# Queries read the state at their block's end; biases move into a last weight row; one gelu activation per expert block

## The chip, the cores and the metric

The kernel runs on one core of one Trainium2 chip, in one launch. A core has five engines that each work through an instruction queue of their own, in order: TensorE (PE in the profile) multiplies matrices into PSUM, VectorE (DVE) and ScalarE (ACT) work on SBUF and PSUM, GpSimd (POOL) works on SBUF and issues indirect DMAs, SyncE (SP) issues the other DMAs. They wait for each other through semaphores. The metric is the device time of an execution in microseconds (us), all data in float32.

## The reference

Input x has 8 sequences of 512 steps with 128 features. Two layers follow each other, each as attention and feed-forward part with a residual connection, each part fed with a layer norm of x (mean removed, divided by the standard deviation, no gain).

```python
x = x + ssm(_layernorm(x))          # gated linear recurrence along the steps
x = x + (_layernorm(x) @ W[idx] + b[idx])   # one of 8 matrices, picked from logits
x = x + delta(_layernorm(x))
x = x + moe(_layernorm(x))
```

The third is the delta rule. With 16 heads of 8 features, each step and head updates a state S of 8x8 and reads it after the update:

```python
normed = (x - mu) * rsqrt(var + LN_EPS) * ln_g + ln_b
q, k, v, beta_pre = split(normed @ w_qkvb + b_qkvb)   # k is then normalised
def step(S, inp):
    q_t, k_t, v_t, beta_t = inp
    retrieval = einsum('bhij,bhj->bhi', S, k_t)
    S = S + einsum('bhi,bhj->bhij', beta_t * (v_t - retrieval), k_t)
    o_t = einsum('bhij,bhj->bhi', S, q_t)
    return (S, o_t)
out = x + scan_out @ w_out + b_out
```

The fourth is a mixture of experts. A router (128x8) and softmax pick two of eight experts for each of the 4096 rows; an expert is `gelu(x @ w1 + b1) @ w2 + b2` with 512 hidden features, and the two results are added with the softmax weights.

## The kernel before

**Tiles and stages.** The 512 steps are cut into 32 tiles of 16 steps; a tile holds the 8 sequences of these steps, 128 rows. Eight chunks of 4 tiles go through the stages: `first_layers` (the first part in `scanned` and `ssm_out`, the second in `linear`), `delta_in` (norm, q, k, v, beta and per-block matrices of the delta rule), `delta_rule`, `route` (router). Chunks are gathered into groups of 1, 2, 2, 2 and 1 (`GROUPS`), and `experts` runs once for each group.

**The order** is written out: every operation is first recorded with a number, and `ORDER`, a table of numbers, says in which order they are emitted (`ordered`, line 189), so on each engine's queue too. Which PSUM bank an operation gets follows in `ordered` from which one was free longest. Because operations go through a recorder, most instructions carry its line, L335, in the profile; groups are told apart by their tiles.

**The delta rule.** A tile is worked in four blocks of 4 steps, 128 blocks in all, one after the other, since each needs the state that the one before leaves. Rows of SBUF are (head, feature) pairs. The state and the terms added to it lie in PSUM (`st`, two banks in turn). A block is six instructions on DVE (lines 1308 to 1337): the product `so` = (queries, keys of this block) x state, 128x512; its reduction over the key features, with the values already written beside it, gives `w`, value less retrieval; a product with a 4x4 matrix for each sequence and head (`tmat`, made in `delta_in` from keys and beta) and its reduction give the four steps' updates `u`; keys times `u` into `st`, and its reduction is the next state. Keys carry the minus sign that is needed.

The queries' half of `so` is q times the state at the block's *start*. What the updates inside the block add to a step's output is made up by correction planes `qkp`: dot products of a step's query with the keys of the steps of its block, four planes (own step, others), made in `delta_in` on POOL (products), PE (sums over a head's features with `head_ones`) and ACT (copies into `qk_planes`). POOL multiplies them with the updates shifted against each other (`upd`), and PE adds the eight planes of `so` and the four of `qkp` times `wo` into the tile's output; from tile 8 on POOL first adds the planes of `so` in pairs, and from tile 28 on the `qkp` planes onto them (`PRESUM`). DVE then adds the result to `base` and has x3.

Keys and queries reach the block's layout by way of DRAM: `scratch<-knq` stores a chunk, `kq<-scratch` loads a tile, keys and queries apart, each copied to the eight rows of a head; `kq` has two buffers.

**Biases.** In `linear` the chosen bias `bsel` is added to x1 on POOL, and DVE adds the product in PSUM to it. In `experts` w1 and b1 are copied in DRAM into `w1b_dram`, rows of 516 numbers: 512 weights and 4 columns of bias.

**Experts.** DVE computes each row's place in a table sorted by expert. POOL scatters the normed rows (`places<-xne`, 128 rows per indirect DMA). A group of n tiles takes 15 (n = 4) or 23 (n = 8) blocks of 128 rows, 99 in all. For a block SP loads the expert's `w1b` (four buffers), PE makes four 128x128 products `ph`, ACT four gelus of 128x128, each with its bias column, and PE four products with w2 (`po<-w_sb,hid`, or `in<-`). Four blocks' results are stored, POOL gathers them back by row (`back<-results`), multiplies with the weights and adds (`fin`) for the chunks of the first three groups; for the last two groups DVE does this in one instruction per tile. `out_rows` then goes to the output.

Of the kernel before, what the change touches and what calls it, by code (L numbers as in the profile page):

```python
# [16 lines left out]
P = 128  # L17
# [52 lines left out]
class Plan:  # L70
# [118 lines left out]
    def ordered(self):  # L189

        order, loaded, freed = [], None, list(range(-len(self.banks), 0))
        for at, number in enumerate(ORDER):
            op = self.ops[number]
            for b in op.begins:
                b.index = min(b.choice, key=freed.__getitem__)
                freed[b.index] = len(ORDER)
            for b in op.ends:
                b.users -= 1
                if b.users == 0:
                    freed[b.index] = at  # L200
            switch = op.table if op.table and op.table != loaded else None
            loaded = switch or loaded
            order.append((op, switch))
        return order
# [154 lines left out]
def _cost(engine, name, n, kw):  # L359
# [28 lines left out]
    0, 9, 63, 116, 57, 1, 11, 69, 67, 40, 3, 18, 46, 4, 13, 61, 2, 5, 32, 44, 8, 23, 62, 48, 6, 7, 59, 49, 22, 29,  # L388
    20, 330, 411, 50, 75, 109, 12, 15, 70, 45, 16, 17, 51, 43, 110, 54, 47, 71, 10, 26, 41, 68, 72, 111, 27, 33, 112,
    14, 19, 60, 325, 113, 25, 337, 73, 42, 21, 35, 114, 65, 115, 24, 34, 117, 64, 125, 331, 118, 119, 74, 344, 126,  # L390
    127, 120, 323, 36, 124, 128, 132, 79, 133, 121, 52, 122, 53, 135, 123, 338, 129, 134, 351, 130, 76, 37, 131, 137,
    136, 39, 326, 358, 139, 138, 365, 327, 78, 328, 140, 141, 142, 89, 84, 90, 148, 149, 147, 143, 86, 329, 150, 154,
    155, 144, 145, 157, 151, 146, 156, 152, 153, 159, 158, 382, 161, 160, 379, 163, 164, 162, 380, 165, 171, 169,
    170, 28, 381, 383, 172, 166, 177, 176, 384, 167, 168, 179, 178, 385, 173, 386, 174, 181, 175, 180, 387, 182, 183,
    87, 333, 80, 185, 186, 332, 388, 446, 184, 334, 191, 335, 77, 187, 193, 192, 81, 389, 336, 199, 188, 352, 194,
    189, 390, 190, 200, 198, 195, 203, 196, 197, 201, 391, 58, 392, 204, 202, 208, 106, 91, 340, 205, 108, 207, 85,
    209, 206, 345, 88, 213, 31, 396, 214, 210, 215, 211, 107, 221, 393, 212, 83, 38, 216, 220, 416, 394, 395, 858,
    217, 222, 398, 218, 223, 92, 225, 219, 399, 224, 226, 93, 397, 227, 339, 400, 229, 94, 228, 366, 230, 235, 30,
    236, 237, 55, 56, 231, 359, 401, 243, 242, 372, 238, 232, 402, 233, 245, 234, 244, 403, 239, 240, 247, 241, 95,
    246, 96, 404, 341, 248, 249, 97, 98, 251, 252, 99, 342, 250, 253, 100, 101, 258, 259, 257, 254, 415, 260, 255,  # L400
    66, 405, 264, 265, 102, 256, 267, 266, 261, 406, 262, 269, 263, 268, 104, 270, 447, 271, 103, 354, 273, 274, 407,
    448, 272, 451, 275, 279, 449, 280, 82, 452, 276, 281, 287, 277, 105, 278, 453, 286, 408, 282, 288, 289, 409, 283,
    284, 291, 285, 290, 410, 292, 293, 450, 353, 413, 295, 347, 355, 454, 294, 356, 296, 455, 297, 412, 299, 346,
    460, 298, 348, 417, 414, 349, 418, 456, 461, 466, 300, 462, 420, 303, 301, 304, 467, 308, 305, 302, 457, 309,
    468, 312, 421, 313, 310, 422, 306, 423, 311, 314, 307, 419, 357, 469, 315, 316, 458, 317, 350, 373, 343, 318,
    367, 424, 360, 319, 320, 368, 459, 321, 322, 470, 361, 483, 324, 463, 425, 427, 464, 471, 579, 426, 375, 428,
    374, 429, 440, 465, 430, 431, 432, 435, 433, 436, 434, 472, 437, 438, 439, 362, 363, 441, 369, 442, 473, 443,
    444, 445, 474, 514, 581, 513, 475, 376, 515, 516, 517, 377, 482, 518, 476, 519, 523, 520, 477, 529, 521, 530,
    522, 478, 531, 526, 532, 378, 527, 480, 525, 533, 524, 364, 583, 534, 479, 580, 484, 370, 481, 536, 485, 535,
    537, 582, 487, 542, 538, 539, 528, 544, 540, 543, 541, 545, 548, 550, 546, 553, 551, 584, 585, 549, 586, 587,  # L410
    646, 554, 588, 488, 489, 490, 547, 555, 491, 648, 556, 561, 492, 647, 494, 557, 507, 558, 1193, 493, 689, 371,
    690, 495, 562, 593, 496, 486, 559, 563, 552, 560, 565, 564, 497, 566, 574, 498, 567, 594, 568, 569, 595, 570,
    649, 500, 502, 575, 650, 571, 599, 591, 572, 499, 573, 651, 501, 652, 503, 653, 600, 504, 505, 654, 592, 601,
    655, 656, 657, 658, 602, 659, 660, 506, 661, 603, 508, 662, 589, 663, 664, 509, 665, 510, 590, 666, 511, 667,
    668, 675, 732, 669, 676, 688, 512, 677, 730, 596, 678, 604, 576, 1128, 1127, 597, 679, 670, 680, 671, 577, 681,
    672, 616, 673, 731, 691, 578, 598, 682, 674, 692, 693, 1130, 694, 695, 605, 683, 696, 684, 685, 697, 1129, 686,
    1131, 698, 699, 606, 687, 700, 1132, 701, 1133, 1137, 702, 1134, 703, 1143, 607, 1144, 704, 705, 1140, 706, 608,
    1141, 707, 1136, 708, 1135, 709, 615, 609, 710, 1145, 717, 774, 1196, 711, 718, 712, 1146, 772, 719, 713, 1197,
    720, 714, 721, 1147, 722, 773, 733, 715, 610, 1148, 734, 716, 735, 736, 723, 737, 724, 1149, 738, 725, 1150, 726,
    739, 611, 740, 1151, 741, 613, 742, 743, 727, 1152, 744, 614, 745, 1153, 1156, 746, 1154, 747, 728, 748, 1155,  # L420
    1157, 617, 1138, 729, 1158, 1164, 749, 1167, 1195, 1165, 750, 1194, 1162, 751, 1159, 752, 612, 759, 1160, 753,
    760, 754, 761, 1163, 762, 755, 1168, 763, 1262, 756, 1161, 764, 765, 775, 1169, 1139, 766, 1261, 1198, 757, 1199,
    776, 1170, 1175, 618, 758, 1260, 1200, 1201, 1171, 1166, 777, 1202, 767, 778, 768, 779, 769, 1207, 780, 1176,
    781, 770, 1177, 782, 1172, 1208, 783, 620, 1209, 784, 785, 1173, 786, 1179, 1203, 1213, 787, 1174, 788, 1178,
    1214, 1205, 789, 1204, 1180, 790, 791, 792, 1181, 793, 1182, 794, 801, 1304, 1183, 771, 802, 1302, 795, 803,
    1184, 621, 796, 804, 797, 805, 1185, 798, 622, 799, 1303, 806, 1186, 1263, 623, 624, 619, 807, 1264, 1187, 808,
    1206, 625, 1215, 626, 1188, 1536, 627, 800, 1265, 1216, 1266, 1267, 628, 640, 814, 809, 1268, 1190, 1269, 1142,
    629, 1217, 810, 1270, 1189, 1271, 1211, 630, 1272, 634, 1273, 1274, 631, 1210, 1218, 1275, 635, 632, 1276, 633,
    1277, 636, 1278, 1212, 637, 1279, 638, 811, 1280, 639, 1281, 1219, 1191, 1282, 641, 642, 1346, 1283, 812, 1284,
    1289, 643, 1285, 1290, 1286, 1291, 1537, 1345, 644, 1305, 1292, 1287, 1293, 1220, 1294, 1306, 1295, 1307, 645,  # L430
    1221, 1308, 1230, 1470, 1538, 1222, 1309, 1539, 813, 1296, 1192, 1310, 1540, 1541, 1288, 1471, 1542, 1223, 1543,
    1311, 1544, 1473, 1472, 1312, 1224, 1297, 1313, 1298, 1474, 1314, 1545, 1315, 1225, 1316, 1550, 815, 1344, 1226,
    1317, 816, 1299, 1318, 1227, 1475, 1319, 1479, 1320, 1321, 1478, 1228, 1322, 817, 1551, 1323, 1556, 1229, 1324,
    1331, 1388, 1552, 1325, 1332, 1326, 1333, 1557, 1300, 1327, 1334, 818, 1335, 1476, 1328, 1387, 1336, 1558, 1386,
    1337, 1231, 1329, 1338, 1477, 1546, 1232, 1330, 1559, 1486, 1487, 1488, 819, 1489, 1347, 1234, 1339, 1560, 1340,
    1348, 1341, 1490, 1342, 1349, 1350, 1233, 1572, 1351, 1547, 1480, 1235, 1352, 1236, 1237, 1353, 1238, 1354, 822,
    1355, 1548, 1561, 1239, 1481, 1241, 1499, 2282, 1240, 1549, 1356, 1242, 1357, 1491, 1554, 1358, 1359, 1553, 1243,
    1360, 1493, 1361, 1492, 1362, 1254, 1363, 1555, 1364, 1494, 1365, 1500, 1562, 1366, 1495, 1367, 1373, 1507, 1368,
    1374, 1496, 1369, 1573, 1370, 1371, 1244, 1483, 1375, 1343, 1372, 1376, 1389, 1497, 1377, 1378, 1245, 1390, 1379,
    1380, 1498, 1563, 1605, 1391, 1381, 1392, 1382, 1393, 1383, 1384, 1564, 1394, 1512, 823, 1508, 1395, 1484, 1396,  # L440
    1565, 2286, 1397, 820, 1301, 1398, 1246, 1510, 1385, 1566, 1399, 1501, 1400, 1247, 1401, 821, 1604, 1509, 824,
    1567, 1402, 825, 826, 1568, 1403, 1404, 1511, 827, 1405, 1406, 1570, 1482, 828, 1407, 1502, 829, 830, 831, 1408,
# [1444 lines left out]
```

## Time and profile before

| | us |
|---|---|
| time, median of 3 (lowest to highest) | 690.27 (689.65 to 692.26) |
| the profiled execution, own time | 689.16 |
| its span, first to last instruction | 687.4 |
| mean granted TensorE clock | 0.868 |
| first and last `so` product begin | 99.5 and 561.6 |
| last reduction of the delta rule ends | 565.0 |
| last output of a tile added to x3 | 576.1 |
| last scatter of rows begins | 621.8 |

The profile lists busy time by engine and by groups of like instructions: engine, operation, what is written from what, shapes and count, then total busy us and mean ns of one, then idle time ahead of them with what ended it. PEld is TensorE's loading of weights, beside PE. A float32 product counts as two PE records. The longest groups of each engine are, in us busy: PE `ph<-xbT,w1b` 124.5, ACT `hid<-ph,w1b` 116.4, DVE `so<-kq,st` 87.8 and the two reductions of the delta rule 63.7 and 63.0, POOL the scatter 63.0 and the gather 61.3. A wait named in the profile is the one that ended last.

### The profile page before, as it was taken

How to read it: one execution, taken by the hardware profiler on the slowest of the kernel's cores; microseconds unless marked ns; L12 is line 12 of the kernel's file. 1: busy time of each engine (PE TensorE's matmuls, PEld its weight loads, DVE VectorE, ACT ScalarE, POOL GpSimd, SP SyncE). 2: the span in 40 equal slices, each digit the busy share in tenths (PEclk: the TensorE clock that was granted, in tenths of full speed). 3: DMA queues.
4: the chain of work that ended last, by engine and by line, in shares of the span. 5: the costliest groups of instructions: out<-in, count | busy, mean ns of one | idle time of the engine just before them, and what ended most of it. 6: DMA issues, size and time to landing. Idle time of an engine off the chain costs nothing. (4 is left out here: it accounts for less than half of the span.)

```text
span 687.4 us, 10830 instructions
## 1 busy us (share of the span) xinstructions
PE 513.5 (75%) x2948; PEld 402.5 (59%) x2948; DVE 504.4 (73%) x1351; ACT 480.3 (70%) x1129; POOL 484.3 (70%) x522
## 2 busy tenths in 40 slices
PE   4976575776667786894779787886988788969960
PEld 3763233444435454583748565765778787969850
DVE  5786759989999989988699999997899970300121
ACT  2565687757786779897698799966878457836640
POOL 4164563695589879698869886976788687774443
PEclk9966577888987589988799979997999899999995
DMA  3894062343242654656268666564697767877761
GB/s 88 248 263 136 0 169 62 103 110 78 61 108 61 186 137 122 157 146 161 80 155 234 164 153 178 151 191 145 179 242 206 207 189 214 272 210 219 223 197 46
DMA packets 94977, 107.48 MB, mean 156 GB/s; under 512 B 8667, under 2 KB 68006, under 8 KB 94918
## 3 DMA queue, kind: packets, MB, share of 16 engines
q1 hardware_dynamic: 89616, 97.97, 52.4%
q0 software_dynamic: 4160, 8.53, 4.3%
q8 instruction: 25, 0.41, 0.3%
q10 hardware_dynamic: 1142, 0.29, 0.2%
q14 instruction: 34, 0.28, 0.2%
HBM read 84.93 MB, written 27.61 MB: 164 GB/s over the span
## 5 line engine op out<-in xcount | busy, mean ns | idle before, releaser
L335 ACT ACTIVATE hid<-ph,w1b 128x128 f32<-128x128 f32 x396 | 116.4, 380 | 45.3 <-PE ph L335 29.2
L335 PE MATMUL ph<-xbT,w1b 128*128 128x128 f32 x792 | 124.5, 287 | 18.5 <-DMA w1b<-w1b_dram 12.7
L335 PEld LDWEIGHTS ph<-xbT,w1b 128*128 128x128 f32 x792 | 108.0, 199 | 31.9 <-issue 17.9
L1601 PE MATMUL po<-w_sb,hid 128*128 x608 | 98.4, 284 | 5.2 <-ACT hid L335 4.2
L1601 PEld LDWEIGHTS po<-w_sb,hid 128*128 128x128 f32 x608 | 85.0, 198 | 14.5 <-ACT hid L335 8.0
L335 DVE TENSOR_TENSOR so<-kq,st 128x512 f32<-128x512 f32 x128 | 87.8, 686 | 6.7 <-PE po L335 2.0
L335 POOL DMA_INDIRECT back<-results,small_dest x64 | 61.3, 958 | 38.8 <-issue 15.9
L1539 POOL DMA_INDIRECT places<-xne,small_dest x64 | 63.0, 984 | 18.9 <-issue 14.3
L304 ACT ACT_TABLE_LOAD x56 | 71.8, 1283 | 1.0
L335 DVE TENSOR_REDUCE st<-st 128x64 f32<-128x320 f32 x128 | 63.7, 498 | 3.8
L335 DVE TENSOR_REDUCE st<-so 128x32 f32<-128x320 f32 x128 | 63.0, 492 | 4.0
L335 PE MATMUL po<-wo,so 128*128 128x128 f32 x248 | 49.7, 331 | 20.9 <-DVE so L335 10.1
L335 PEld LDWEIGHTS po<-wo,so 128*128 128x128 f32 x248 | 43.3, 239 | 31.1 <-DVE so L335 12.5
L335 DVE TENSOR_TENSOR st<-kq,st 128x256 f32<-128x256 f32 x128 | 54.6, 426 | 3.6
L335 POOL TENSOR_TENSOR qkp<-qkp,upd 128x512 f32<-128x512 f32 x32 | 38.9, 1215 | 15.3 <-ACT upd L335 12.9
L335 PE MATMUL in<-b,wqkvb 128*128 128x512 f32 x64 | 41.0, 741 | 9.6 <-ACT b L335 4.3
L335 PE MATMUL in<-f,wT 128*128 128x512 f32 x64 | 42.3, 756 | 7.1 <-ACT f L335 3.8
L335 DVE SCALAR_TENSOR_TENSOR fin<-back,small_weight,fin 128x128 f32<-128x128 f32 x16 | 5.0, 351 | 56.7 <-DMA w1b<-w1b_dram 44.1
L335 POOL TENSOR_TENSOR f<-f,f 128x512 f32<-128x512 f32 x24 | 30.4, 1273 | 19.9 <-ACT f L335 19.9
L335 DVE TENSOR_REDUCE st<-prod 128x32 f32<-128x128 f32 x128 | 37.5, 293 | 7.8 <-ACT upd L335 2.4
L335 POOL TENSOR_TENSOR so<-so 128x512 f32<-128x512 f32 x24 | 30.5, 1271 | 13.2 <-PE in L335 6.4
L335 DVE TENSOR_TENSOR prod<-tmat,st 128x128 f32<-128x128 f32 x128 | 36.6, 286 | 4.0
(300 smaller groups left out, 1301.0 us busy)
## 6 DMA issues: line engine op xcount, KB each, us to landing
kq<-scratch SPq DMA_DIRECT2D x64, 512.0 KB
w1b<-w1b_dram SPq DMA_DIRECT2D x99, 258.0 KB
xb<-places SPq DMA_DIRECT2D x21, 256.0 KB
results<-yb SPq DMA_DIRECT2D x21, 256.0 KB
scratch<-knq SPq DMA_DIRECT2D x16, 256.0 KB
places<-yb SPq DMA_DIRECT2D x2, 1472.0 KB
w1b_dram<-in_L_ffn_w_dram SPq DMA_DIRECT2D x1, 2048.0 KB
u_rows<-in_L_attn_u_dram SPq DMA_DIRECT2D x7, 256.0 KB
```

The costliest lines, as they stand in the source:

```text
L304: self.hw.scalar.preload_act_table_set(switch)
L335: return method(*(on(x) for x in args), **{k: on(x) for k, x in kw.items()})
L1539: rows_out = hw.gpsimd.indirect_dma_start(out=table[0 : nblk * P, :], out_offset=bass.IndirectOffsetOnAxis(ap=at, axis=0), in_=src, in_off ...
L1601: return hw.tensor.matmul(out_.on(nc.banks), lhsT=src, rhs=w2_f[:, bass.ds(at + c * P, P)], start=(c == 0), stop=(c == NHB - 1),)
```

## The change

1. **The delta rule's order within a block.** `so` is computed at the block's end, from the state after its updates. The queries in it are this block's, the keys those of the *next* block, whose retrieval it prepares. So the stored keys and values are shifted by one block (`STEP` = 32 columns): a chunk's keys go to `scratch` in three stores, 96 columns of them into the last tile's place, and the next chunk's first 32 columns complete that tile. `first_keys` and `first_block` provide for the first block, and the very last `so` has queries alone. `delta_in` of a chunk is recorded one chunk earlier than before.
2. **Three correction planes.** With the state read at the end, the own step needs none, and later steps of the block are subtracted: planes 0 to 2, with a minus sign, and updates shifted the other way. The product of queries and keys on POOL, its 128x512 product on PE and its copy on ACT are gone, and a tile's output adds three `qkp` planes (one, from tile 28 on).
3. **Biases.** A normed row sums to zero, so its last feature is minus the sum of the others. The last weight row is subtracted from the other 127 (`differences`, a product with `less_last`), the last feature is set to 1, and the bias becomes the last row: for w1 and `wr` (no bias there) and `wsel`. For w1 this is done once at the start: 1 MB each into the two `kq` buffers, eight products of 128x512, copies by DVE and ACT, a store to `w1b_dram`, and b1 over every last row. `w1b` has rows of 512 numbers.
4. **x2** is made, from the second chunk on, by adding x1 in PSUM with an identity product and one copy on ACT, in place of DVE's addition.
5. **Gelu** of a block is one activation of 128x512.
6. **Weighting** of gathered rows for the first three groups is done by ACT, 128x128 each, instead of POOL.
7. `ORDER` is another one, and the banks are listed in `BANKS`.

```diff
@@ ordered
-        order, loaded, freed = [], None, list(range(-len(self.banks), 0))
+        order, loaded, banks = [], None, iter(BANKS)
...
-                b.index = min(b.choice, key=freed.__getitem__)
...
+                b.index = int(next(banks))
@@ setup
+    def differences(src):
+        pt = mm_tile()[:, 0 : src.shape[1]]
+        nc.tensor.matmul(pt, lhsT=less_last, rhs=src, start=True, stop=True)
+        return pt
...
-    nc.sync.dma_start(w1b_dram[:, 0 : NHB * P], w1.rearrange("e d f -> (e d) f"))
...
+    for h in range(2):
+        w1_sb = ptile([P, half_e, FW], "kq", 2)
+        nc.sync.dma_start(w1_sb, w1[h * half_e : (h + 1) * half_e].rearrange("e p f -> p e f"))
+        for e in range(half_e):
+            copied = nc.scalar.copy if e % 2 else nc.vector.tensor_copy
+            copied(w1_sb[:, e], differences(w1_sb[:, e]))
+        nc.sync.dma_start(
+            w1b_dram[h * half_e * P : (h + 1) * half_e * P].rearrange("(e p) f -> p e f", p=P), w1_sb
+        )
+    nc.sync.dma_start(w1b_dram.rearrange("(e p) f -> e p f", p=P)[:, P - 1, :], b1)
...
+    nc.tensor.matmul(pt, lhsT=less_last, rhs=wsel, start=True, stop=False)
+    nc.tensor.matmul(pt, lhsT=only_last, rhs=bsel, start=False, stop=True)
+    nc.vector.tensor_copy(wsel, pt)
@@ linear
-        x1b = ptile([P, n, D], "f", FIRST)
-        nc.gpsimd.tensor_add(x1b, x1, over_tiles(bsel, n))
+        xn = ptile([P, n, D], "f", FIRST)
+        nc.gpsimd.memset(xn[:, :, D - 1 :], 1.0)
+        normalised(x1, rstd, shift, tiles_of(xn[:, :, 0 : D - 1]), leads=leads)
...
-        nc.vector.tensor_add(x2, tokens_out(xT, wsel), x1b)
+        if leads:
+            nc.vector.tensor_add(x2, tokens_out(xT, wsel), x1)
+        else:
+            nc.scalar.copy(x2, tokens_out(xT, wsel, onto=x1))
@@ delta_in
+        before_first = scratches[(g - 1) % 2][1, SIZES[g - 1] - 1, :, QN - STEP :] if g else first_keys
+        nc.sync.dma_start(before_first, kn[:, 0:STEP])
+        nc.sync.dma_start(tiled(scratch[0, 0:NT]), qn.rearrange("p (q c) -> p q c", c=QN))
+        nc.sync.dma_start(
+            tiled(scratch[1, 0 : NT - 1]), kn[:, STEP : STEP + (NT - 1) * QN].rearrange("p (q c) -> p q c", c=QN)
+        )
+        nc.sync.dma_start(scratch[1, NT - 1, :, 0 : QN - STEP], kn[:, STEP + (NT - 1) * QN :])
...
-        nc.gpsimd.tensor_mul(pa, qn, kn)
...
-        nc.scalar.copy(planes[:, 3, :], project_md(head_ones, pa))
@@ delta_rule, in a block
-                nc.vector.tensor_mul(so_v[:, :, :, ts], kq_v[:, :, ts], state)
-                nc.vector.tensor_reduce(w.rearrange("p b t -> p (b t)"), so_r[:, ts], AX.XY, ALU.add)
+                so_r = so_before[:, DH * QN :].rearrange("p (x c e) -> p c x e", c=QN, e=2)
+                nc.vector.tensor_reduce(w.rearrange("p b t -> p (b t)"), so_r[:, before_], AX.XY, ALU.add)
...
                 nc.vector.tensor_reduce(terms(n + 1)[:, :, BL], sum_n, AX.X, ALU.add)
+                so_before, k_before = now, keys_of(kq)
+                sides_ = 1 if last and k == QB - 1 else 2
+                state = terms(n + 1)[:, :, BL].unsqueeze(1).unsqueeze(3).to_broadcast([P, sides_, DH * B, BL])
+                xs = slice(0, sides_ * DH // 2)
+                nc.vector.tensor_mul(so_v[:, xs, :, ts], kq_v[:, 0 : sides_ * DH, ts], state)
@@ delta_rule, after a tile
-                outs += [mine[:, d, :] for d in range(BL)]
+                outs += [mine[:, d, :] for d in range(BL - 1)]
@@ experts
-            for c in range(NHB):
-                cs = slice(c * P, (c + 1) * P)
-                nc.scalar.activation(
-                    hid[:, cs], ph[:, cs], AF.Gelu_apprx_tanh, bias=w1b[:, NHB * P + c : NHB * P + c + 1]
-                )
+            nc.scalar.activation(hid, ph, AF.Gelu_apprx_tanh)
...
-                    weight = weights[:, c].unsqueeze(2).to_broadcast([P, n, D])
-                    nc.gpsimd.tensor_mul(back[c], back[c], weight)
+                    for i in range(n):
+                        nc.scalar.mul(back[c][:, i], back[c][:, i], weights[:, c, i : i + 1])
@@ the chunks' loop
+    x2s = {g: first_layers(g) for g in range(2)}
+    delta_ready(0)
+    first_block(ready[0][1])
+    for g in range(NG):
+        if g + 1 < NG:
+            delta_ready(g + 1)
```

## The prediction

> **What bounds the kernel now.** The engine totals come first: no engine fills the span, so shares decide nothing and the stages have to be found.
>
> ```profile
> span 687.4 us, 10830 instructions
> PE 513.5 (75%) x2948; PEld 402.5 (59%) x2948; DVE 504.4 (73%) x1351; ACT 480.3 (70%) x1129; POOL 484.3 (70%) x522
> DVE  5786759989999989988699999997899970300121
> ```
>
> The DVE row of the forty slices (17.2 us each) has three parts: six slices of setup, a plateau of eights and nines to slice 33, then almost nothing. The plateau is the delta rule. Its first `so` product starts at 99.5, its last reduction ends at 565.0 (timeline of DVE). Busy time in four stretches, cut where the delta rule begins and ends, where PE hands out the last tile (575.9) and where PE's last expert block ends (666):
>
> ```profile
> core 0: us, PE busy (x) PEld busy (x) DVE busy (x) ACT busy (x) POOL busy (x), PEclk, DMA share, GB/s
> 99.00:563.00 464.00, 356.74 (x1985) 273.30 (x1985) 418.40 (x1058) 358.96 (x799) 360.88 (x387) 0.87 0.55 147
> 563.00:575.90 12.90, 10.09 (x84) 9.61 (x85) 2.16 (x6) 6.26 (x22) 11.05 (x14) 1.00 0.71 201
> 575.90:666.00 90.10, 79.15 (x653) 75.30 (x651) 13.01 (x57) 58.00 (x180) 54.44 (x55) 0.98 0.78 227
> 666.00:687.40 21.40, 1.12 (x2) 0.29 (x2) 3.32 (x9) 0.56 (x2) 7.56 (x8) 0.58 0.25 71
> ```
>
> In the plateau DVE is busy 418.4 of 464.0 us, PE, ACT and POOL 77 to 78%. From 575.9 to 666 PE leads, 79.2 of 90.1 us. The last 21.4 us are results, gathers and stores. The list of DVE's waits in the plateau says what DVE lacks:
>
> ```profile
> DVE x L335 <- PE in L335: 9.5, 5, 2.7
> DVE x L335 <- PE po L335: 2.9, 1, 2.9
> DVE st L335 <- ACT upd L335: 2.4, 1, 2.4
> DVE so L335 <- PE po L335: 2.0, 2, 1.2
> ```
>
> Columns are total us, times, longest. With the entries under 1 us these are 19.1 us. The other 26.5 of the 45.6 idle us are some 25 ns after each of 1058 instructions. So the plateau is a DVE stage with little to squeeze except work removed from DVE and these waits, and the tail is a PE stage whose length is the number of expert blocks still to do.
>
> **The recurrence, part by part.** One of the 128 steps is six DVE instructions: `so` 0.686, reduction of `so` 0.492, `prod` 0.286, its reduction 0.293, product into `st` 0.426, reduction 0.498, together 2.68 us. Moving `so` to the step's end leaves the same cyclic sequence with the same shapes (the diff's widths do not change). Only the last is half as wide: 0.686 less 0.426 (the 128x256 product), 0.3 us. No gain here.
>
> What leaves DVE is the 128x512 addition to x2 for seven of eight chunks (group: busy us, mean ns):
>
> ```profile
> L335 DVE TENSOR_TENSOR x<-in,f 128x512 f32<-128x512 f32 x8 | 5.5, 684 | 5.5 <-PE in L335 5.5
> ```
>
> 7 x 0.684 = 4.8 us. In the changed instruction order some small statistics, an output addition and a tile of `base` fall inside the plateau instead of beside it, about 3 us by their rows. Plateau work: **-2 us**. Its 19 us of waits I leave unchanged (see the rivals).
>
> **Startup.** Here the change adds: eight 128x512 products on PE (the row of 128x512 products by `wT` gives 2 x 0.66 busy us each), four copies on DVE and four on ACT (0.6 to 0.7 each), and w1 makes two trips instead of one DRAM-to-DRAM copy. Most lies beside the squaring loop. Two things reach the first step. The last DVE copy into a `kq` buffer stands just ahead of the chain that builds `tmat` (+0.7). SP then waits for that copy before it stores the buffer's 1 MB, and behind this store stand the keys of tile 0 and of the first block, which use the same buffer. By the timeline of before that copy would end near 95. With 1 MB at the 250 to 300 GB/s the setup reaches, plus about 2.4 us for a transfer (scratch store at 88.7, load behind it at 91.1), twice, the first keys land near 103.5 to 104.5; `tmat` and `prod` would let the `st` product start at about 102.9. **+2 us**; it could be 0 (keys early) or +8 (w1's stores at half that rate, squarings held up).
>
> A rule speaks against the key stores. The Trainium skill, "DMA: Bandwidth & Descriptors", section Specifications, puts the smallest transfer for line rate at 512 B; below it there is read-modify-write. The old stores have 512 B pieces, the new ones also 384 B and 128 B. The trace shows 2.4 us from issue to the dependent load for 512 B. If the short ones take twice that, startup gains 2 us more and the later chunks nothing, since their keys are stored well before use (chunk 1: stored at 132.6, needed near 149 in the new order). I stay with 2.4; the difference is in the range.
>
> **ACT, POOL, PE: relief beside the path.** Four biased gelus of 128x128 take 1.14 us together in the timeline of ACT (start, length):
>
> ```profile
> 560.99 1.14 ACT L335 ACTIVATE hid<-ph,w1b 128x128 f32<-128x128 f32 x4 [0.20 <-ACT hid L335]
> ```
>
> Two groups (busy us, mean ns of one) give the other prices:
>
> ```profile
> L335 ACT COPY yb<-po 128x512 f32<-128x512 f32 x16 | 9.6, 601 | 0.6 <-DMA results<-yb 0.4 <-PE po L1601 0.2
> L304 ACT ACT_TABLE_LOAD x56 | 71.8, 1283 | 1.0
> ```
>
> A 128x512 gelu is not in the trace. Bounds: the copy from PSUM, 0.601, and the same size with a bias column (`vals`), 0.695. I take 0.61, as the bias goes: 99 x (1.14 - 0.61) = -52 us. Ten table loads fewer in the new order: -12.8 by the row. "ScalarE: Activation LUTs", section What ACT_TABLE_LOAD costs, counts 2.66 us a switch, a drain included, so -26.6. The trace has the next activation 1.29 us after a load's start (576.76, then 578.05): I use 1.28. Either way nothing of it ends a stage. The fourth plane's copy goes (8 x 0.58 = -4.6), seven x2 copies come (+4.1), 40 weightings of 128x128 come (between 0.31, the plain copy, and 0.50, scale and bias columns; at 0.35, +14), startup and split copies +4. ACT: about **-47 of 480**.
>
> POOL: `bsel` addition 8 x 1.275, query-key product 8 x 1.4, `back` weighting 10 x 1.04, correction product 32 x about 0.2 (1.215 now; 1.095 is the row of a 128x384 product, 0.91 would be three quarters): -38, plus small memsets: **-36 of 484**.
>
> PE: in the plateau -24 correction matmuls (0.36 each), -8 products of 128x512 (1.2 each), +7 with the identity (1.3 each): -9 us, before what the order moves.
>
> **The tail: where this becomes time.** In PE's instruction order I count what follows the last output matmul of tile 31: 347 matmuls before, 298 in the changed kernel. In expert blocks 60.2 of 99 against 65.8 are done by then. Before, the 347 take 575.9 to 666, 0.26 us each with all their waits. 49 x 0.26 = **-12.7 us**. The plateau must take them: 5.6 blocks x 2.4 = +13 us of PE, against -9 above, into a stage where PE is idle for 107. ACT even loses work there with more gelus in it (64 of 0.61 against 58 x 1.14).
>
> POOL must keep up too. Ten of the gathers (1.25 us apart) and two `fin` additions move ahead of tile 31's correction product, and its six weightings after it vanish, so the last scatter starts about 22 us after that product against 39 (567.5 to 606.8). The routing before that scatter has 71 matmuls in front of it instead of 99: destinations ready about 21 us after the output, not 27. Expert rows of the last group are then in SBUF near +36 us, and PE, with some 163 matmuls to do first, wants them near +42. It fits with 6 us to spare.
>
> From the end of the recurrence to tile 31's output PE needs 10.9 us now, of which about 2.5 is POOL; the rest is expert work and a load of `w1b` that stand ahead of it. In the new order five expert matmuls lie between the planes. But `so` itself comes later now: POOL's 1.27 and 0.7 follow it. I take 8: **-3 us**. The end's 21.4 us stay, being eight gathers and two stores.
>
> Sum: startup +2, plateau -2, hand-over -3, tail -12.7 = -15.7. From the profiled execution, 689.16 (span 687.4 and 1.8 around it): 673.5. The median shown is 690.27, 1.1 above it, so I forecast **674 us**.
>
> **Rivals.**
> 1. *The waits go with the relief* (0.20). DVE's 19 us hang on PE output that waits for POOL and ACT; with both 8 to 10% lighter and `w1b` buffers freed by PE instead of by gelu, two thirds of them and 5 us of the tail's `w1b` waits (10.2 in total) go: 674 - 13 - 5 = 656. Against it: a new order uses up the slack it is given.
> 2. *DVE stalls on tile outputs* (0.14, the slow side). The addition of a tile's output to x3 stands in DVE's queue, and behind it the next recurrence step. Its mean distance behind the tile's last `so` is 1.2 tiles before and 0.8 in the new order; 14 of the 31 tiles ahead of the last are at half a tile or less, against 6. The query read now ends with the step, so POOL's sum (1.27) and PE's five matmuls start later. A missed one costs 2.7 us by the wait list. Six eat the gain; ten give 674 + 27 = 701.
> 3. *PE cannot take the 5.6 blocks early* (0.10). It is busy 77% at clock 0.87, and in-order waits may hold it: tile 31's output is then later by what the tail saves, 13 us: 687 to 690. For it: 12.7 us before `ph` are put down to `w1b`; against it: these loads now wait for gelu to free their buffer, later for PE alone.
> 4. *As forecast*, 0.56, own range 664 to 684.
>
> **Numbers.** What a measurement can tell here is about 0.5%, 3.4 us, so faster is below 686.8. Faster: 0.56 + 0.20 and a part of rival 3 = 0.78; same 0.08; slower 0.14. The range takes most of rivals 1 and 3, startup's +8 and stalls up to four: 656 to 692.
>
> **What would show it.** Startup: second step's `so` starts at 105 to 106 (103.6 before). Plateau: DVE busy lower by 2 and named waits near 19; over 35 is rival 2, under 10 rival 1. Gelu of 128x512 at 0.58 to 0.66. Hand-over: last output 8 us after DVE's end; over 15 is rival 3. Tail: 298 matmuls in about 77 us. The forecast is wrong at its root if the tail stays near 90 us with fewer matmuls, which would make `w1b` loads or POOL its limit.

## The result, and the profile after

The changed kernel takes **683.53 us** (median of 17 runs, 680.56 to 689.91); the kernel before took 689.75 us beside it (17 runs). The ratio is 0.9917, with an interval from 0.9894 to 0.994: faster by 0.8%, where 2.3% were forecast. The profiled execution has a span of 680.4 us, 7.0 less than before.

The page of the changed kernel first: span, busy times, DVE in forty slices of 17.0 us.

```profile
span 680.4 us, 10437 instructions
PE 511.5 (75%) x2920; PEld 399.3 (59%) x2920; DVE 504.9 (74%) x1350; ACT 432.8 (64%) x873; POOL 444.9 (65%) x517
DVE  7788589999978999999759999977999865030121
```

ACT and POOL are lighter by 47.5 and 39.4 us, as costed. But DVE's row has deeper holes: a 7 at slice 12, a 7 and a 5 at 20 and 21, two 7 at 27 and 28, where before had a 6 at 20 and a 7 at 28. Busy time by stretch of the changed kernel, cut where the delta rule begins and ends on DVE, at the last tile's output and where PE's expert blocks end:

```profile
core 0: us, PE busy (x) PEld busy (x) DVE busy (x) ACT busy (x) POOL busy (x), PEclk, DMA share, GB/s
99.98:575.15 475.17, 364.59 (x2041) 282.49 (x2041) 415.58 (x1047) 323.22 (x645) 340.30 (x389) 0.85 0.58 152
575.15:583.70 8.55, 8.26 (x74) 8.07 (x73) 0.00 (x0) 4.16 (x9) 7.71 (x8) 1.00 0.87 242
583.70:660.00 76.30, 67.68 (x557) 65.80 (x556) 11.09 (x56) 38.33 (x75) 38.74 (x40) 0.96 0.73 214
660.00:680.40 20.40, 2.07 (x2) 0.50 (x2) 3.41 (x9) 0.56 (x2) 7.58 (x8) 0.51 0.26 74
```

| stage, profiled executions | before | after | change | forecast |
|---|---|---|---|---|
| to the `so` that the second step needs | 103.6 | 100.0 | -3.6 | +2 |
| from there to DVE's end of the delta rule | 461.4 | 475.2 | **+13.8** | **-2** |
| from there to the last tile's output | 11.1 | 8.6 | -2.5 | -3 |
| from there to the end | 111.3 | 96.7 | -14.6 | -12.7 |
| sum | | | -6.9 | -15.7 |

The tail and the start came better than forecast, the hand-over 0.5 us short of it. The plateau took back two thirds of what they brought. DVE's work in it is as before (415.6 us, in the same cut 416.0 before); its idle time rose from 45.5 to 59.6. The list of DVE's waits in this stage (total us, times, longest) says for what:

```profile
DVE x L330 <- PE po L330: 14.2, 3, 10.5
DVE prod L330 <- POOL tmat L330: 8.8, 2, 6.7
DVE so L330 <- PE in L330: 5.9, 1, 5.9
DVE small_runf L330 <- PE po L330: 1.9, 1, 1.9
```

With the small entries 34.1 us, where before had 19.1: 15 more. They are few and long: 10.5 us at 347, 6.7 at 462, 5.9 at 550, 3.3 at 569, 2.1 at 221. Three of the groups give prices that the forecast had to estimate:

```profile
L299 ACT ACT_TABLE_LOAD x46 | 59.0, 1283 | 0.8
L330 ACT ACTIVATE hid<-ph 128x512 f32<-128x512 f32 x99 | 57.6, 597 | 47.2 <-PE ph L330 44.2 <-PE po L1668 2.6
L330 POOL TENSOR_TENSOR qkp<-qkp,upd 128x384 f32<-128x384 f32 x32 | 29.2, 914 | 16.0 <-ACT upd L330 15.7
```

**What stands ahead of the longest wait.** The timeline of POOL in the changed kernel, around the wait that ends at 347:

```profile
335.38 0.98 POOL L1606 DMA_INDIRECT places<-xne,small_dest  x1 [0.17 <-issue]
336.67 0.96 POOL L1606 DMA_INDIRECT places<-xne,small_dest  x1 [0.30 <-issue]
337.94 0.96 POOL L1606 DMA_INDIRECT places<-xne,small_dest  x1 [0.31 <-issue]
339.21 0.96 POOL L1606 DMA_INDIRECT places<-xne,small_dest  x1 [0.30 <-issue]
340.20 1.27 POOL L330 TENSOR_TENSOR so<-so 128x512 f32<-128x512 f32 x1
```

and that of DVE:

```profile
335.84 0.69 DVE L330 TENSOR_TENSOR so<-kq,st 128x512 f32<-128x512 f32 x1
347.07 0.29 DVE L330 TENSOR_TENSOR x<-po,base 128x128 f32<-128x128 f32 x1 [10.54 <-PE po L330]
```

`so<-so` is the pair sum of tile 15, ready to run when DVE has that tile's last `so`, at 330.6. It runs at 340.2, behind a row of scatters, 1.27 us each, and one sum for a later chunk. PE then makes the output from 341.5 to 347, in turns with expert matmuls, and DVE, whose addition of this output stands two steps behind the tile, has waited since 336.5. The wait's name says PE, but PE was waiting for POOL, and POOL, in this row, for no other engine: its queue held scatters for the experts, wanted much later, in front of a sum wanted at once. Before the waits at 462 and 221 it is the same with `tmat` of a new chunk.

These scatters do not stand there in `ORDER`. That `ORDER` sets every queue is true of four engines; on GpSimd it is true only up to the scatters. This queue is left to the framework's scheduler, with each instruction tied behind the one emitted before it (`keep_in_program_order`). Scatters are also declared independent of each other; where two follow each other, this seems to take the tie away again (the program shows the result, not the reason). Compared instruction by instruction, up to eight scatters stand further ahead than written in the changed kernel (eight at tile 15's pair sum, six at the `tmat` near 462), up to six in the kernel before. That suggested the first experiment.

### The profile page after: what moved, and what is told of

Read it like the earlier page. It is cut to its first block, busy times and chain, and to the rows that moved or that the text cites. A ratio compares the mean times of both kernels' runs of the same rounds, so it can differ in the third digit from the quotient of the medians.

```text
span 680.4 us, 10437 instructions
## 1 busy us (share of the span) xinstructions
PE 511.5 (75%) x2920; PEld 399.3 (59%) x2920; DVE 504.9 (74%) x1350; ACT 432.8 (64%) x873; POOL 444.9 (65%) x517
## 4 chain that ended last, share of the span: by engine, by line
DVE 52%; PE 12%; POOL 11%; DMA 10%; issue 6%; ACT 5%; SPq 2%; ACTq 1%; POOLq 0%; DVEq 0%
DVE st L330 24%; DVE so L330 10%; DVE prod L330 4%; POOL places L1606 4%; DMA back<-results,small_dest 3%; PE in L330 3%; PE ph L330 3%; PE po L330 3%; DMA results<-yb 2%; PE po L1668 2%; POOL back L330 1%; POOL b L330 1%; DVE x L330 1%; DVE sp L330 1%; DMA w1b<-u_rows 1%
## 5 line engine op out<-in xcount | busy, mean ns | idle before, releaser
L330 PE MATMUL ph<-xbT,w1b 128*128 128x128 f32 x792 | 127.2, 289 | 20.2 <-ACT hid L330 9.0
L330 PEld LDWEIGHTS ph<-xbT,w1b 128*128 128x128 f32 x792 | 109.9, 202 | 31.1 <-ACT hid L330 12.5
L1668 PE MATMUL po<-w_sb,hid 128*128 x648 | 105.3, 286 | 10.3 <-ACT hid L330 4.0
L1668 PEld LDWEIGHTS po<-w_sb,hid 128*128 128x128 f32 x648 | 90.2, 199 | 18.2 <-ACT hid L330 6.8
L330 ACT ACTIVATE hid<-ph 128x512 f32<-128x512 f32 x99 | 57.6, 597 | 47.2 <-PE ph L330 44.2
L330 PE MATMUL po<-wo,so 128*128 128x128 f32 x288 | 57.2, 340 | 32.5 <-POOL so L330 19.4
L330 PEld LDWEIGHTS po<-wo,so 128*128 128x128 f32 x288 | 51.4, 248 | 46.9 <-POOL so L330 21.9
L330 PE MATMUL in<-f,wT 128*128 128x512 f32 x64 | 40.0, 716 | 8.8 <-ACT f L330 4.3
L330 PE MATMUL in<-b,wqkvb 128*128 128x512 f32 x64 | 39.3, 711 | 5.6 <-ACT b L330 2.4
L330 POOL TENSOR_TENSOR qkp<-qkp,upd 128x384 f32<-128x384 f32 x32 | 29.2, 914 | 16.0 <-ACT upd L330 15.7
```

The lines of the kernel that those rows point to most:

```text
L330: return method(*(on(x) for x in args), **{k: on(x) for k, x in kw.items()})
L1668: return hw.tensor.matmul(out_.on(nc.banks), lhsT=src, rhs=w2_f[:, bass.ds(at + c * P, P)], start=(c == 0), stop=(c == NHB - 1),)
```

## The experiments

Three theories are tried. **A**: the scatters that run ahead make the plateau's loss. **B**: the new order does; output additions stand too close behind their tile (rival 2 of the forecast). **C**: POOL and PE cannot do more in the plateau, and waits only change their place. Two more, **D** and **E**, come up for one place near the end: a few instructions stand wrongly there, or PE and ACT are late there whatever the place of these few.

### GpSimd in the written order

Nothing else differs; the other four engines' orders are the same instruction for instruction.

```diff
 if op.engine == "gpsimd":
     self.tc.keep_in_program_order(made)
+    scatter = op.emit.__qualname__.endswith("scatter.<locals>.emit")
+    for other in fixed if scatter else fixed + loose:
+        queue = mybir.DependencyInfo(mybir.DependencyClass.NoSync, mybir.DependencyReason.DATA)
+        self.tc.add_manual_dep(made.ins, other, queue, reason="the order written")
+    if scatter:
+        loose.append(made.ins.name)
+    else:
+        fixed, loose = [made.ins.name], []
```

> The changed kernel with one difference: GpSimd keeps exactly the written instruction order, so no scatter of tokens stands further ahead in its queue than written (as built, up to eight scatters of some 1.27 us stand ahead of a pair sum `so` or of `tmat`, at the places where VectorE has its long waits). Theory A, scatter bursts cause the plateau's loss: VectorE's named waits between 100 and 575 us fall from 34 to under 18, the 10.5 us wait for a tile output near 347 and the 6.7 us wait for `tmat` near 462 go, and the time falls from about 683.5 to 668-673. Theory B, the new order itself is at fault (output additions stand too close behind their tile, whatever the scatters do): the additions still wait, in sum over 10 us, and the time is 680-685. Theory C, VectorE's waits are set by what POOL and PE can do in the plateau: the waits turn up at other places with the same sum, time 682-686.

> The kernel before, with GpSimd held to the written order in the same way. Its bursts are 13 and 11 scatters long, but its VectorE waits there are 2.9 us at most, 19 in all. Theory A: the order costs this kernel less, 0 to 5 us, so 685-690. Theory B and C: no change, 689-691. If it gains as much as the changed kernel, the bursts are no difference between the two and explain nothing of the missed forecast.

Measured: the changed kernel 694.83 us, the kernel before in written order 730.53. But the kernel before, unaltered, took 745.26 us on this chip. Ratios to it: 0.9321 (0.9278 to 0.9364) and 0.9801 (0.9756 to 0.9846); for the kernel before this is 14.7 us less, where theory A had expected 0 to 5. In the trace of the first, the waits at 221, 347 and 462 are gone. The absolute times of the expectations could not be judged here, and the changed kernel was missing beside them; so:

> The changed kernel itself, unaltered, so that it stands on the same chip as the others (on the chip of the first three runs the kernel before took 745 us, not 690). If this chip is like the first one: 0.992 of the kernel before. If it is like the second one[...], all theories leave the ratio open; the ratios of the other runs to this one are what is compared.

> The changed kernel with GpSimd held to the written order, again, beside the unaltered one. On the second chip the four waits of VectorE at 221, 347, 462 and 569 us (22.6 us in the changed kernel's trace) were gone. Theory A: 14-22 us under after_again, about 662-670 us where the kernel before takes 690. Theories B and C: within 4 us of it.

On such a chip again (kernel before 740.2): unaltered 710.32, in written order 693.94, so 16.4 us less, inside A's 14 to 22. At last a chip like the first:

> The changed kernel with GpSimd in the written order, once more, in case this chip is one like the first (kernel before near 690 us): step by step it was 13.6 us ahead of the changed kernel by step 117[...]. Theory A then gives 683.5 - 13 to 20 = 664 to 670 us, ratio 0.96 to 0.972 to the kernel before. On a chip like the second: 0.93 to 0.94 again.

> The kernel before with GpSimd in the written order, beside it. By step 96, where both chips agree to 0.2 us, it was 10.2 us ahead of the kernel before. If bursts cost both kernels, and the changed one more, this one gains 5 to 10 us on a chip like the first (680 to 685 us, ratio 0.985 to 0.993), and less than after_pinned_f gains over the changed kernel; on a chip like the second 0.975 to 0.985 again.

**664.49 us** for the changed kernel in written order (ratio 0.9634, 0.9597 to 0.9671) and 676.47 for the kernel before in written order (0.9806, 0.9768 to 0.9844), beside 689.45. It is the version that beats both kernels. The order takes 19.0 us off the changed kernel (from its 683.53) and 13.0 off the kernel before: more than the 5 to 10 expected there, so most of what the scatters cost is common to both kernels. Tile 15's pair sum in the changed kernel in written order:

```profile
327.32 0.96 POOL L1615 DMA_INDIRECT places<-xne,small_dest  x1 [0.30 <-issue]
328.78 1.26 POOL L339 TENSOR_TENSOR so<-so 128x512 f32<-128x512 f32 x1 [0.49 <-DVE so L339]
```

It waits for DVE alone, half a microsecond, and the addition behind it, at the same place of DVE's queue, for 0.84 us. The waits of DVE in the plateau, changed kernel in written order:

```profile
DVE so L339 <- PE in L339: 6.1, 1, 6.1
DVE x L339 <- PE po L339: 2.5, 3, 1.0
DVE small_runf L339 <- PE po L339: 1.8, 1, 1.8
```

and of the kernel before in written order:

```profile
DVE x L344 <- PE in L344: 0.8, 3, 0.4
DVE so L344 <- PE po L344: 0.7, 2, 0.5
```

In all 15.0 and 3.0 us, against 34.1 and 19.1 as built. Theory B falls: the additions are where they were, and wait 2.5 us in sum. C falls for the plateau as a whole, since the sum did not stay. Theory A holds for most, but it holds for both kernels. The stretches of the changed kernel in written order (plateau, then hand-over):

```profile
101.04:556.66 455.62, 359.51 (x2046) 277.75 (x2045) 414.97 (x1047) 321.99 (x644) 338.74 (x389) 0.87 0.60 159
556.66:565.14 8.48, 7.88 (x68) 7.57 (x67) 0.00 (x0) 4.40 (x10) 7.67 (x8) 1.00 0.78 229
```

and of the kernel before:

```profile
102.11:549.16 447.05, 341.83 (x1985) 262.88 (x1986) 417.29 (x1050) 354.28 (x791) 360.50 (x388) 0.91 0.57 152
549.16:560.96 11.80, 9.68 (x82) 9.09 (x80) 0.29 (x2) 6.49 (x23) 10.10 (x12) 1.00 0.64 186
```

So the scatters cost the changed kernel 19.6 us of plateau (475.2 to 455.6) and the kernel before 14.4 (461.4 to 447.05). Of the 13.8 us, 5.2 are this difference; **8.6** are left. They lie at the end: step by step, the two kernels in written order are level within 0.3 us at step 120, and 8.6 apart when the delta rule ends.

### One burst put back

Eight scatters (1874 to 1889) moved in `ORDER` ahead of tile 15's pair sum (2491), in the kernel in written order, and nothing else:

```diff
-    2489, 1135, 2679, 2490, 2491, 2715,
+    2489, 1135, 2679, 2490, 1874, 1879, 1877, 1886, 1887, 1889, 1888, 1884, 2491, 2715,
```

> The changed kernel with GpSimd held to the written order, as the partner of the next run on its chip. 0.93 to 0.94 of the kernel before if this chip is like the second one; if it is like the first one, theory A expects 0.96 to 0.975 (683.5 less 14 to 20 us over 690), theories B and C 0.985 to 0.995.

> As the run before it, and one burst put back by hand: eight scatters (8 x 1.27 = 10.2 us of GpSimd's queue) ahead of the pair sum `so` of tile 15, nothing else. Theory A: VectorE's wait `x <- PE po` near 350 us is 9 to 11 us again, the waits for `tmat` stay away, and the time rises by 6 to 11 us. If the step after it catches up (the stall is slack that is paid back in the next wait): 0 to 3 us. Theory B and C: no change.

699.33 against 693.32 us (kernel before 744.27; ratios 0.9422, 0.9389 to 0.9455, and 0.9321, 0.9289 to 0.9352): 6.0 us slower, at the lower edge of A's 6 to 11. The waits with the burst:

```profile
DVE x L339 <- PE po L339: 10.2, 1, 10.2
DVE so L339 <- remote: 9.0, 1, 9.0
```

The wait on outputs is 10.2 us again, where the partner has one of 2.2 at the same place, and those for `tmat` stay away. Of the 8.0 us more, 6.0 reach the end: here eight scatters, 10.2 us of GpSimd's queue, cost 6.0. (The second line is a wait at step 121 that the partner has too, 9.0 us on this chip.)

### The rest: step 121

In written order one long wait is left, 6.1 us at step 121, where `so` may not be overwritten until PE has read it for tile 28. Two of those matmuls stand behind a row of expert matmuls. First these two were moved forward (on both kinds of chip), then also ScalarE's copy `upd` (4272), which had become the next to be late, to ahead of the five instructions for experts that begin with 3147. The first of the two edits:

```diff
-    3809, 4225, 4203, 2206, 3848,
+    3809, 4225, 4203, 4204, 4205, 2206, 3848,
...
-    3121, 3112, 4204, 3844, 3122, 4205, 3126,
+    3121, 3112, 3844, 3122, 3126,
```

> As after_pinned, and two matmuls of tile 28's output (the third and fourth of `in<-wo,so`) moved in TensorE's order from behind the expert blocks to directly behind the second one, so that the step at 549 us (5.9 us of waiting `so <- PE in`) finds its buffer read. If this wait is TensorE's order: another 3-6 us less than after_pinned_again. If the transfer of the keys ends just behind it (on the second chip the wait was 9 us with the matmuls done 2.4 us before its end): 0-2 us less.

> The changed kernel with GpSimd in the written order, as the partner of the next two on their chip: 0.960 to 0.968 of the kernel before on a chip like the first, 0.93 to 0.94 on one like the second.

> As its partner, with two output matmuls of tile 28 moved ahead of expert blocks in TensorE's order. On the second chip the wait at step 121 went, and one of 6.1 us (`st <- ACT upd`) came three steps later. Theory D, the wait is the place of a few instructions: the time falls by 4 to 6 us. Theory E, the expert blocks that were moved into this part hold TensorE and ScalarE up, and VectorE waits wherever it next needs one of them: within 2 us of the partner, and 4 to 6 us of waits turn up within ten steps behind step 121.

> As the run before it, and ScalarE's copy `upd` of tile 30 moved ahead of five of ScalarE's instructions for expert blocks (xbT, x3T, yb, two gelus). Theory D: this wait goes too, and the time is 4 to 8 us under the partner. Theory E: the next wait takes its place (a tile output, or the last tile's), VectorE's end and the time stay within 2 us of the partner.

On the chip like the second: 689.94 us (six runs from 680.20 to 694.16) against 693.94 (691.92 to 699.09), the wait at step 121 gone and one of 6.1 us on `upd` three steps later. The two profiled runs took 692.99 and 693.74, with plateaus of 460.6 and 459.9, so the profiles cannot show where a gain would come from; with this spread it stays open whether there is one. On the chip like the first (kernel before 689.19): 665.25, 663.44 and 665.32 us, ratios 0.963, 0.9629 and 0.9647 with intervals of 0.004 to either side: no difference. DVE's waits from 525 us to the end of the delta rule, for the partner:

```profile
DVE so L339 <- PE in L339: 4.9, 1, 4.9
DVE so L339 <- PE po L339: 1.3, 1, 1.3
DVE x L339 <- PE po L339: 1.0, 1, 1.0
DVE st L339 <- ACT upd L339: 0.8, 1, 0.8
```

with PE's two matmuls moved:

```profile
DVE st L339 <- ACT upd L339: 3.9, 1, 3.9
DVE so L339 <- PE po L339: 2.9, 1, 2.9
DVE x L339 <- PE po L339: 1.0, 1, 1.0
```

and with `upd` moved too:

```profile
DVE so L339 <- PE po L339: 6.0, 1, 6.0
DVE x L339 <- PE po L339: 1.0, 1, 1.0
DVE st L339 <- ACT upd L339: 0.9, 1, 0.9
```

8.0, 7.8 and 7.9 us. The wait moves from one name to the next and keeps its sum: D falls, and it is not the place of these two or three instructions. What E says in its place is argued: PE has more to do in this part. From the 111th step to the end of the delta rule, the changed kernel in written order and the kernel before in written order:

```profile
490.33:556.66 66.33, 59.23 (x449) 53.66 (x448) 54.00 (x146) 34.86 (x76) 51.17 (x64) 0.97 0.85 234
489.24:549.16 59.92, 47.86 (x383) 43.99 (x382) 55.62 (x154) 39.56 (x112) 47.32 (x56) 1.00 0.79 211
```

PE is busy 11.4 us longer in the same steps, 89% of the stretch for 80%. That the expert blocks moved here are the cause was not tried by taking them out. A rival was not tried either: the weighting of gathered rows, now in ScalarE's queue (point 6 of the change), waits there for its gathers, 10.1 us in six waits between 490 and 557, and one of these holds PE up for 1.6 us.

### Gelu in four pieces again

```diff
-            nc.scalar.activation(hid, ph, AF.Gelu_apprx_tanh)
+            def gelus():
+                full = ph.on(nc.banks) if isinstance(ph, Bank) else ph
+                for c in range(NHB):
+                    cs = slice(c * P, (c + 1) * P)
+                    made = hw.scalar.activation(hid[:, cs], full[:, cs], AF.Gelu_apprx_tanh)
+                return made
+            nc.add("scalar", gelus, [ph], [hid], _cost("scalar", "activation", N, {}), 0.0, SETS[AF.Gelu_apprx_tanh])
```

> The changed kernel with the gelu of a block in four activations of 128x128 again, without bias, in the same place of the order; nothing else differs. ScalarE gets 99 x about (1.0 - 0.60) = 40 us more work. If ScalarE's relief lies beside the path, as the forecast costed it, the time stays within 3 us of 683.5. If the relief is what carries the gain (the gelu stands between PE's two halves of a block in the tail, 33 blocks there), the tail grows by up to 33 x 0.4 = 13 us and the kernel is back at 690-697.

> The gelu of a block in four activations of 128x128 again (295 ns each, so 99 x (1.18 - 0.60) = 58 us of ScalarE's time at most, 20 us in the busy time, where they overlap), otherwise the changed kernel. If ScalarE's relief lies beside the path: within 3 us of after_again. If it carries the gain: 6 to 13 us slower, as slow as the kernel before.

719.35 us where the kernel before took 745.26 (0.9644), and 715.06 beside the changed kernel's 710.32: 4.7 us slower, ratios 0.9645 (0.9603 to 0.9687) and 0.9591 (0.9547 to 0.9634), whose intervals overlap, so the difference is not clear of noise. ACT's busy time rises by 17.9 us (450.6 against 432.7). It lies between the two expectations. In the profiles the difference is spread over all stages (plateau 1.2, tail 1.2, hand-over 0.9, the start 1.7, which is within that mark's scatter, see below), nowhere the 13 us of a gelu that leads the tail. What the single gelu spares ScalarE lies beside the path, or nearly.

### The kernel before on the second chip

> The kernel before, unaltered, for a profile on this chip beside the one of the first. It tells where the 50 us lie by which it is slower on the second chip, and whether VectorE's waits in the plateau are its 19 us there too. If the chip is slower in transfers alone: instruction lengths as before (686 ns for a `so` product), plateau within 5 us of the 461 us of the first, and the difference in the tail.

742.16 us. Step by step it is within 0.2 us of the first chip's trace up to step 96; from there it falls behind, 11.7 us by step 100 and 19.6 by step 124. The tail, from the last tile's output on, is 142.4 us instead of 111.3. So the expectation that the plateau is within 5 us was wrong; that the tail carries most was right (31 us).

## Why the forecast was wrong, and where it was right

**The step that failed** is the one for the plateau: "Its 19 us of waits I leave unchanged (see the rivals)". They became 34.1 us, and the stage came 13.8 us longer instead of 2 shorter. DVE's own work in it fell by 0.4 us instead of 2. What the runs put in the place of this step:

- The waits of before were not part of the structure that could be carried over. In written order 16 of the 19 us go. They depended on where scatters stood in GpSimd's queue, which differs from program to program and which neither `ORDER` nor the diff shows. As built, it cost the kernel before 14.4 us of plateau and the changed one 19.6. This part is shown: the order was held, and one burst was put back. The forecast's own page had a trace of it. Its row was read as eights and nines but has a 6 at slice 20, and there DVE waits 2.9 us, until 332.5, for an output whose pair sum stood behind four scatters more than written.
- In written order the plateau is 8.6 us longer than before, of which about 8 lie in waits around steps 121 to 126. Where they lie is shown, their cause is not; that PE is behind there fits its load. The sum for PE in the plateau, +13 - 9 = +4 us, was too small: busy time rose by 10.1 us as built (354.5 to 364.6) and by 17.7 in written order (341.8 to 359.5, with 61 matmul records more and 335 ns for a mean one instead of 329). "It is busy 77%" was true of the mean and no reason at the end, where it is 89%.

**Startup**, forecast +2, came at -3.6. The DVE copy that was to end "near 95" ended at 87.3, and the chain for the first keys ran 2.5 us earlier (stored at 86.2, before at 88.7), so the keys were in use at 99.0 and not at 103.5, without a wait; what their shorter pieces cost by themselves, no run separates. These 5.6 us in the forecast's favour are luck: had the start come as forecast, the stages would sum to -1.3 and not to -6.9. This term is also less sharp than it looked: in thirteen profiles of kernels that share the changed kernel's start, on chips of both kinds, the mark lies between 99.97 and 102.12.

**Hand-over and tail** were right in size, and the tail in its cause too: fewer matmuls at the price of before. The last output follows DVE's end by 8.6 us (8 forecast). The 298 matmuls took 76.3 us, 0.256 each (about 77 forecast); the end behind them 20.4 (21.4). The tail gained 14.6 for 12.7. In written order it gained 18.1 (115.5 to 97.5). One reading behind it was wrong: 606.8 is where the first of the last eight scatters begins, and the last begins at 621.8. In the changed kernel the first of these eight begins 29 us behind tile 31's correction product (578.5 to 607.7), not 22. It cost little: PE waits 1.1 us in the tail for a load of such rows.

**The prices.** Gelu of 128x512 is 0.597 us (0.61 taken), ten table loads fewer at 1.283 (as taken), ACT -47.5 (-47). POOL -39.4 for -36: the product with three planes is 0.914 us, at the lower bound of its range and not at the value in between, 32 x 0.1 us more. None of these terms was in the sum. Gelu's was tested (4.7 us, not clear of noise); the others were not tested by themselves.

**The rivals.** Rival 2 named the right instruction, `x<-po,base` in DVE's queue, and its own mark, over 35 us, was all but reached. Its price and its cause were wrong: two long waits on outputs (10.5 and 3.3) instead of ten of 2.7, and the distance from the tile was not the cause, since at the same distance they wait 2.5 us in all. Rival 3, PE that cannot take the blocks, fits the last 8 us, for its 13, but it was not shown; its own mark, a last output over 15 us after DVE's end, did not come (8.6), since the waits came ahead of that end. Rival 1, waits that go with the relief, did not occur: GpSimd had 39 us less to do, and DVE waited longer for it.

**The change by itself**, both kernels in written order, is 664.49 against 676.47: **-12.0 us**, of the forecast -15.7. As built 6 us of it are lost to the scatters' places.

## What to carry to other kernels

A share of busy time does not say what an in-order queue does to one urgent instruction: look at what stands directly ahead of each sum or matrix that the leading engine waits for, engine by engine, in the built program and not in the list that was meant to order it. A wait list of before is a property of one order; when the order changes it is to be worked out anew; here one miss behind a burst cost 10.5 us of waiting, where the longest old wait on an output was 2.9. When a wait is removed by moving its instruction, sum the waits over the next ten steps before believing it: if the sum stays, as here at 8 us, it was not the place of that instruction.

## What was not expected of the hardware

The same programs took 740 to 745 us on some chips and 689 on others. On DVE, ACT and POOL instructions last the same (a `so` product 686 ns in both), and the first 96 steps of the kernel before are the same to 0.2 us; the changed one is 3 us later from step 60 on. Later the kernel before loses 19.6 us in the plateau and 31 in the tail there, the changed one 7.8 (483.0 for 475.2) and 22.5 (119.2 for 96.7). So the change brings 4.1% there (0.9591) against 0.8%. TensorE differs: in the tail of the kernel before its granted clock is 0.82 for 0.98, an expert product `ph` takes 302 ns for 285, and it is busy 85.1 us for 79.0, so 6 of the 31 us are there. Slower transfers do not show: the packets of the main DMA queue take 360 us of the 16 engines' time on both (52.4% of 687.4 us, 48.6% of 740.4). Four of the longest waits there, DVE's of 7.0 us to 472 and 8.2 to 572 and PE's of 12.1 to 652 and 10.5 to 694, end in or just behind rows of indirect DMAs on GpSimd. Whether these hold other transfers up, and why the kernel before suffers more, these runs do not settle. So a ratio holds for the kind of chip it was taken on, and partners have to run on the same one.
